# Two graph layers on one core: four small re-orderings at the seams of the stages

## Chip, cores, metric

One core of one Trainium2 chip runs the whole program; the other cores are idle. The metric is the device time of one execution in microseconds (us), as a median of several runs. Below, the engines are called TensorE (PE in the profile), VectorE (DVE), ScalarE (ACT), GpSimd (POOL) and SyncE (SP). SyncE computes nothing: it issues DMA transfers. ScalarE and GpSimd can issue transfers too, each in its own instruction stream.

## What is computed

The inputs are `x` (8 batches, 2048 rows, 256 columns, float32) and a sparse 2048 x 2048 matrix `adj` with a full diagonal. Cut to what matters, the reference is:

```python
# layer 0
deg   = rowsum(adj + I) + colsum(adj + I) - diag(adj + I)
A_hat = (adj + I) * deg**-0.5 [rows] * deg**-0.5 [columns]
h   = relu(batchnorm((A_hat @ x) @ W1.T))        # 512 columns, statistics over all 16384 rows
x   = layernorm(x + batchnorm(h @ W2.T))         # back to 256 columns
# layer 1
q, k, v = split(x @ W)                           # 4 heads of 64
attn = softmax(q @ k.T / 8, only where adj != 0)
x   = layernorm(x + attn @ v)
```

## The kernel before, in words

The 2048 rows are cut into 16 row tiles of 128. Rows with low numbers have many neighbours, the others few. So row tiles 0 and 1 of layer 0, and row tile 0 of layer 1, are done densely; every other row tile goes through lists of its neighbours' numbers: rows of the neighbours are gathered from DRAM by indirect DMA and added up with weights. Five stages follow one another. A recording layer (`manual_schedule`) keeps, on each engine, the order in which the Python program emits instructions, so every engine is a queue in that order.

**Stage 1, column sums and searches (lines 425 to 478).** For each row tile `t`, SyncE loads 128 rows of `adj` into a slot `e` (1 MB; there are 16 slots). ScalarE adds up its rows (L432) and its diagonal (L433), TensorE adds its columns into the PSUM tile `pc` by a product with ones (L451). For `t > 2` the loop also takes two steps from the generator `search_steps`. A search of one row tile is four steps, all on VectorE: it replaces nonzeros of the slot by their column numbers (L224), finds the eight largest of each of 12 or 16 segments (L230, in two steps), and merges these (L235 to L242) into a list of up to 32 neighbours, `nbx`. There are 15 searches, 60 steps: row tiles 2 to 15, then 1. After the loop VectorE copies `pc` to SBUF (`cs`, L464), TensorE transposes it (L467), VectorE combines row sums, diagonal and column sums (L468 to L470), and GpSimd raises the result to the power -1/2 (L146): `dinv`. Then `list_steps` for row tiles 2 and 3 turns the merged lists into gather indices, alternating between VectorE and small TensorE products (L258 to L321, L269, L287).

**Stage 2, dense products (lines 483 to 506).** For each of 16 row blocks `m`, SyncE loads `x` of all batches into `xt` (four buffers), ScalarE scales it by `dinv` (L489) and issues its store to the scratch `xs_d` (L490), and TensorE multiplies it into eight PSUM banks (L493). Each pass takes three more search steps from the generator while any are left, and one or two gathers of `adj` values for the lists of tiles 2 and 3 (L327, GpSimd).

**Stage 3 (to about 600 us)** gathers rows of `xs_d` (L565), adds them up on VectorE (L643) and TensorE (L652), and makes the first linear layer (L393), kept or stored as `h_d`.

**Stage 4 (to about 814 us)** is the second linear layer (`second_linear`), for 16 pairs of row blocks. Pair `n` gives two tiles, `Y[n][0]` and `Y[n][1]`; `store_y(n, r)` stores each with four transfers of 128 KB into the scratch `y_d`, issued by SyncE as soon as VectorE has finished the tile (L738). The order of pairs is 12 to 15, then 0 to 11. So the last pair belongs to blocks 2, 6, 10 and so on of `y_d`. Behind the last stores SyncE issues the loads of the next stage: `wq` (L823), `bias0` (L825), then `yt` from block 0 of `y_d` (L893) and `x1` (L895).

**Stage 5, layer 1 (from about 814 us to the end).** Layer 1's input is normalised and projected for two batches at a time (four such pairs of batches, `p` = 0 to 3; queries, keys and values go to DRAM). A long loop over `n` (4 x 131 = 524 passes) then handles one list entry of 128 rows per pass. Its parts are staggered: pass `n` scores entry `n + 5` (VectorE, L1233 and L1235), takes exponentials of `n + 4` (ScalarE, L1244), weighs the values of `n + 3` (`wv`, on ScalarE by eight instructions at L1260 or on VectorE by one at L1265), and adds up entry `n` for one batch and `n - 2` for the other in PSUM (`add_up`, L1276). The sums `po` of a row tile come from the pool `ps_o`, which has three buffers; the pool `ps_m`, four buffers called `pm`, serves everything else. Other work is hung into the passes by number with `at(n, f, ...)`. When row tile `t` of batch `b` is complete, its tasks are `finish` (divide by the sum of weights, VectorE, L1087 and L1089, which frees the `po` buffer), `residual` (GpSimd, L1096), `out_stats` (VectorE, L856 and L858). After four row tiles (a chunk of 512 rows) come `out_root` (GpSimd, L144 and L146), `out_shift` (VectorE, L866), and `emit` in two halves (ScalarE, two applications L872 each); the second half also issues the store of the whole chunk (512 KB, L1129). In the last pair of batches the entries 518 to 523 form row tile 15, entries 512 to 517 row tile 14. At the very end a small count decides whether a fallback must run (L1357 to L1364, the value is read by all engines at L1677); with these inputs it doesn't.

Of the kernel before, what the change touches and what calls it, by code (L numbers as in the profile page):

```python
# [8 lines left out]
F32 = mybir.dt.float32  # L9
# [9 lines left out]
NHEADS = 4  # L19
# [23 lines left out]
def tile_gcn_then_masked_attention(  # L43
# [15 lines left out]
    nc = tc.nc  # L59
    ENG = mybir.EngineType  # L60
    PSUM = bass.MemoryType.PSUM
    P = 128
# [352 lines left out]
    with tc.tile_pool(name="first", bufs=1, side="right") as fp, tc.manual_schedule(  # L415
        engines=ALL4
    ):
        at = fp.tile([P, DENSE, NT, P], F32, name="at")
        rsum = fp.tile([P, NT], F32, name="rsum")
        diag = fp.tile([P, NT], F32, name="diag")  # L420
        with tc.tile_pool(name="pst", bufs=4, space=PSUM) as pst, tc.tile_pool(
            name="psc", bufs=1, space=PSUM
        ) as psc:
            pc = psc.tile([P, CH], F32, name="pc")
            for t in range(NT):
                s = rows_of[t] = Slot()
                a = s.t
                nc.sync.dma_start(a, adj[t * P : (t + 1) * P, :])
                dj = fp.tile([P, P], F32, name="dj")
                nc.gpsimd.tensor_mul(dj, a[:, t * P : (t + 1) * P], ident)  # L430
                junk = fp.tile([P, N], U8, name="junk")
                nc.scalar.activation(junk, a, AF.Copy, accum_out=rsum[:, t : t + 1])  # L432
                nc.scalar.activation(dj, dj, AF.Copy, accum_out=diag[:, t : t + 1])  # L433
                if t < DENSE:
                    for g in range(NT // 4):
                        ps = pst.tile([P, 4, P], F32, name="ps")
                        for i in range(4):
                            mt = 4 * g + i
                            nc.tensor.transpose(ps[:, i, :], a[:, mt * P : (mt + 1) * P], ident)
                        nc.vector.tensor_copy(at[:, t, 4 * g : 4 * g + 4, :], ps)  # L440
                    if not t:
                        for half in range(2):
                            here = slice(half * NT // 2, (half + 1) * NT // 2)
                            mb = fp.tile([P, NT // 2, P], BF16, name="junk")
                            nc.vector.tensor_scalar(
                                mb, at[:, 0, here], 0.0, MASKED, op0=ALU.is_equal, op1=ALU.mult
                            )
                            nc.sync.dma_start(bias_d[:, here], mb)
                    nc.gpsimd.tensor_add(at[:, t, t, :], at[:, t, t, :], ident)
                for c in range(NCH):  # L450
                    nc.tensor.matmul(  # L451
                        pc[32 * c : 32 * (c + 1), :], ones[:, :32], a[:, c * CH : (c + 1) * CH],
                        start=(t == 0), stop=(t == NT - 1),
                    )
                if not t:
                    rows_of.pop(0).done()
                if t > 2:
                    for _ in range(2):
                        next(search)
            nc.sync.dma_start(w1s, w1t.rearrange("(c p) f -> p c f", p=P))  # L460
            for dst, src in params:
                nc.sync.dma_start(dst, src)
            cs = fp.tile([P, CH], F32, name="junk")
            nc.vector.tensor_copy(cs, pc)  # L464
            pt = psc.tile([P, TPC, P], F32, name="pt")
            for i in range(TPC):
                nc.tensor.transpose(pt[:, i, :], cs[:, i * P : (i + 1) * P], ident)  # L467
            nc.vector.tensor_scalar(over[:, 2, :], diag, 0.0, None, op0=ALU.is_equal)  # L468
            nc.vector.scalar_tensor_tensor(rsum, rsum, 1.0, diag, op0=ALU.add, op1=ALU.subtract)
            nc.vector.tensor_add(  # L470
                rsum.rearrange("p (j i) -> p i j", i=TPC),
                pt.rearrange("p i (j r) -> p i j r", j=NCH)[:, :, :, 0],
                rsum.rearrange("p (j i) -> p i j", i=TPC),
            )
            rsqrt(dinv, rsum, NT, 0.0)
            for t in (2, 3):
                for _ in list_steps(t, pst, "ps"):
                    pass

        ps_a = right.enter_context(tc.tile_pool(name="ps_a", bufs=1, space=PSUM))  # L480
        with tc.tile_pool(name="ps_b", bufs=1, space=PSUM) as ps_b:
            pa = [banks(p) for p in (ps_a, ps_b)]
            for m in range(NT):
                xt = fp.tile([P, N], F32, name="xt", bufs=4)
                nc.sync.dma_start(
                    xt.rearrange("p (b d) -> p b d", b=B),
                    x[:, m * P : (m + 1) * P, :].rearrange("b p d -> p b d"),
                )
                nc.scalar.activation(xt, xt, AF.Copy, scale=dinv[:, m : m + 1])  # L489
                nc.scalar.dma_start(xs_d[m * P : (m + 1) * P, :], xt)  # L490
                for t in range(DENSE):
                    for c in range(QC):
                        nc.tensor.matmul(  # L493
                            pa[t][c], at[:, t, m, :], xt[:, c * CH : (c + 1) * CH],
                            start=(m == 0), stop=(m == NT - 1),
                        )
                for _ in range(3):
                    next(search, None)
                if m < ELL[2] + CAP[2]:
                    gather_value(col0[2] + m)  # L500
                if m < ELL[3] + CAP[3]:
                    gather_value(col0[3] + m)
            for t in (2, 3):
                weights(t)
            for t in range(DENSE):
                scale_rows(t, pa[t])
# [173 lines left out]
    with tc.tile_pool(name="l1", bufs=1, side="right", reuse_waits="tile") as lp, tc.tile_pool(  # L680
# [60 lines left out]

        def store_y(n, r):
            c, i = divmod(pairs[n][0] // 2, TPC)
            for b in range(B // 2):
                nc.sync.dma_start(
                    y_d[(r * B // 2 + b) * NCH + c][:, :, i * P : (i + 1) * P],
                    Y[n][r][:, :, b * P : (b + 1) * P],
                )
# [130 lines left out]
    def attention():  # L879

        with ExitStack() as st:
# [240 lines left out]
            def emit(b, c, half):  # L1122
# [5 lines left out]
                here = slice(parts(b, c)[0], TPC)  # L1128
                nc.sync.dma_start(rows(b, c, out)[:, here], x1.pop((b, c))[:, here])  # L1129

            def emit_rest(b):
                lo.pop((b, "rest")).apply([0])
                nc.sync.dma_start(out[b, :P, :], rest.pop(b)[:, 0, :])
# [137 lines left out]
            def add_up(n, b):  # L1271
                p, g = divmod(n, NG)
                t, r, col, e = tiles[g]
                if not r:
                    po[p, t, b] = ps_o.tile([P, NHEADS, VW], F32, name="po")
                nc.tensor.matmul(  # L1276
                    po[p, t, b].rearrange("p h e -> p (h e)"), oh[n] if e >= 0 else ident,
                    wv[n][:, b, :], start=(r == 0), stop=(r == ELL[t] + CAP[t] - 1),
                )
                if b:  # L1280
                    del wv[n]
                    oh.pop(n, None)
# [39 lines left out]
            for n in range(NALL_G):  # L1322
                p, g = divmod(n, NG)
                t, r, _, _ = tiles[g]
                if n + AHEAD < NALL_G:
                    score(n + AHEAD)
                if n + AHEAD - 1 < NALL_G:
                    exps(n + AHEAD - 1)
                if n + AHEAD - 2 < NALL_G:
                    weigh_values(n + AHEAD - 2)  # L1330
                if n > 1:
                    add_up(n - 2, 1)
                add_up(n, 0)
                if n + LEAD < NALL_G:
                    gather(n + LEAD)
                side_tasks(n)
                if r == ELL[t] + CAP[t] - 1:
                    for b in range(G2):
                        u = n + 1 + 2 * b
                        at(u, finish_block, p, t, b)  # L1340
                        at(u + 1, residual, p * G2 + b, t)
                        at(u + 3, out_stats, p * G2 + b, t)
                        if t % TPC == TPC - 1:
                            u = n + 6 + 2 * b
                            at(u, out_root, p * G2 + b, t // TPC)
                            at(u + 1, out_shift, p * G2 + b, t // TPC)
                            for half in range(2):
                                at(u + 2 + half, emit, p * G2 + b, t // TPC, half)
# [375 lines left out]
```

## Time and profile before

| what | value |
|---|---|
| median of 3 runs | 2200.36 us (2194.45 to 2200.84) |
| the profiled execution's own time | 2182.95 us |
| span of that execution, first to last instruction | 2181.2 us |
| mean granted TensorE clock in it | 0.945 |
| busy: TensorE, VectorE, ScalarE, GpSimd | 1932.5 us (89%), 1735.4 (80%), 1381.4 (63%), 1438.4 (66%) |
| `adj` row tile 15 added into the column sums (L451 ends) | 58.7 us |
| dense products L493 | 88.64 to 200.3 us |
| last product of stage 4 ends, first `yt` load of stage 5 issued | 813.1 us, 817.33 us |
| last list product ends | 2165.6 us |

A row of the timeline gives start (us), duration (us), engine, line, operation, out<-in with shapes, a count, and in brackets how long the engine sat idle before it and what ended the wait. A row of the chain of waits gives start, duration and what the end of the program was waiting for in that stretch. A row of the table by stretches gives, for a stretch of time, the busy time of the five engines with counts of instructions, the TensorE clock that was granted (1.00 is full), the mean busy share of the 16 DMA engines, and GB/s. "SPq" and "ACTq" are the sequencers of SyncE and ScalarE issuing a transfer; "PEld" is TensorE's load of weights.

### The profile page before, as it was taken

How to read it: one execution, taken by the hardware profiler on the slowest of the kernel's cores; microseconds unless marked ns; L12 is line 12 of the kernel's file. 1: busy time of each engine (PE TensorE's matmuls, PEld its weight loads, DVE VectorE, ACT ScalarE, POOL GpSimd, SP SyncE). 2: the span in 40 equal slices, each digit the busy share in tenths (PEclk: the TensorE clock that was granted, in tenths of full speed). 3: DMA queues.
4: the chain of work that ended last, by engine and by line, in shares of the span. 5: the costliest groups of instructions: out<-in, count | busy, mean ns of one | idle time of the engine just before them, and what ended most of it. 6: DMA issues, size and time to landing. Idle time of an engine off the chain costs nothing.

```text
span 2181.2 us, 27900 instructions
## 1 busy us (share of the span) xinstructions
PE 1932.5 (89%) x7590; PEld 1256.5 (58%) x7590; DVE 1735.4 (80%) x3537; ACT 1381.4 (63%) x4145; POOL 1438.4 (66%) x1417
## 2 busy tenths in 40 slices
PE   5599979899999997989999999989999999778785
PEld 1244444454434435657776777767777777566663
DVE  6862898889766662249899998899998999978896
ACT  6222322233354535658878888878797888789886
POOL 2322688888367761146778876777885877777884
PEclk7699989999999998989999999999999999899987
DMA  8698999999738435578999999999998999999994
GB/s 319 198 309 346 414 348 366 371 377 403 298 119 284 157 104 196 198 282 308 347 357 341 354 337 352 351 326 359 329 365 335 344 348 355 364 348 343 336 361 156
DMA packets 259335, 681.89 MB, mean 313 GB/s; under 512 B 25952, under 2 KB 125024, under 8 KB 234208
## 3 DMA queue, kind: packets, MB, share of 16 engines
q0 software_dynamic: 106896, 434.28, 53.2%
q1 hardware_dynamic: 149968, 228.96, 29.9%
q10 hardware_dynamic: 2304, 16.78, 1.8%
q8 instruction: 63, 1.03, 0.2%
q14 instruction: 104, 0.85, 0.1%
HBM read 553.31 MB, written 126.62 MB: 312 GB/s over the span
## 4 chain that ended last, share of the span: by engine, by line
PE 48%; DVE 19%; ACT 13%; DMA 9%; issue 6%; POOL 4%; SPq 0%; another core or an unknown queue 0%; DVEq 0%; ACTq 0%; POOLq 0%
PE pm L1000 9%; PE pa L721 8%; PE po L1276 7%; PE ph L393 7%; ACT wv L1260 6%; PE pa L493 5%; DVE pr L1233 4%; PE pa L652 3%; DVE wv L1265 3%; DVE s L1235 2%; ACT x L872 2%; DMA e<-xs_d,idx 2%; DMA x<-in_x_dram 2%; DMA kg<-kv_d,idx 2%; PE pm L1049 2%
## 5 line engine op out<-in xcount | busy, mean ns | idle before, releaser
L1215 POOL DMA_INDIRECT kg<-kv_d,idx x524 | 558.9, 1067 | 151.4 <-issue 99.5
L1260 ACT ACTIVATE wv<-kg,pw 128x65 f32<-128x65 f32 x1880 | 473.5, 336 | 3.6 <-issue 1.9
L1276 PE MATMUL po<-wv,ident 128*128 128x260 f32 x1536 | 432.9, 395 | 37.1 <-DVE z L1089 18.4
L1000 PE MATMUL pm<-wq,x1t 128*128 128x512 f32 (+1 forms) x1024 | 375.5, 497 | 13.8 <-ACT x1t L945 9.4
L1235 DVE TENSOR_REDUCE s<-pr 128x8 f32<-128x512 f32 x524 | 359.4, 686 | 34.5 <-issue 0.5
L1276 PEld LDWEIGHTS po<-wv,ident 128*128 128x128 f32 x1536 | 286.5, 196 | 101.5 <-issue 52.1
L1233 DVE TENSOR_TENSOR pr<-qb,kg 128x512 f32<-128x512 f32 x384 | 272.5, 710 | 8.6 <-DMA kg<-kv_d,idx 4.1
L1000 PEld LDWEIGHTS pm<-wq,x1t 128*128 128x128 f32 x1024 | 186.8, 193 | 107.0 <-issue 76.5
L565 POOL DMA_INDIRECT e<-xs_d,idx x115 | 158.8, 1381 | 114.9 <-DMA xs_d<-xt 61.7
L1244 ACT ACTIVATE pw<-s,padb 128x8 f32<-128x8 f32 x524 | 155.3, 298 | 119.0 <-DVE s L1235 91.8
L393 PE MATMUL ph<-e,w1s 128*128 128x512 f32 x512 | 226.8, 594 | 1.7 <-ACT e L411 0.9
L1265 DVE TENSOR_TENSOR wv<-kg,pw 128x520 f32<-128x520 f32 x289 | 209.9, 726 | 20.0 <-PE po L1276 13.6
L327 POOL DMA_INDIRECT av<-in_adj_dram,fidx x115 | 164.5, 1431 | 45.5 <-issue 31.4
L1276 PE MATMUL po<-wv,oh 128*128 128x260 f32 x560 | 174.4, 397 | 2.1 <-ACT wv L1260 1.1
L1221 POOL DMA_INDIRECT qg<-q_d,idxq x140 | 141.2, 1008 | 42.7 <-issue 42.4
L398 ACT ACTIVATE h<-ph,b1s 128x512 f32<-128x512 f32 x96 | 66.0, 687 | 156.8 <-PE ph L393 139.1
L643 DVE SCALAR_TENSOR_TENSOR e<-e,wgt,e 128x2048 f32<-128x2048 f32 x70 | 163.9, 2341 | 0.2
L393 PEld LDWEIGHTS ph<-e,w1s 128*128 128x128 f32 x512 | 95.6, 190 | 114.7 <-issue 110.5
L1068 PEld LDWEIGHTS po<-kvr,p 128*128 128x128 f32 x1024 | 136.6, 196 | 43.0 <-ACT p L1057 22.8
L1096 POOL TENSOR_TENSOR x<-z,x 128x256 f32<-128x256 f32 x126 | 125.7, 999 | 51.6 <-DVE z L1089 43.4
L1068 PE MATMUL po<-kvr,p 128*128 128x65 f32 x1024 | 134.1, 275 | 28.2 <-ACT p L1057 19.8
L1049 PE MATMUL pm<-q,kt 128*128 128x256 f32 x512 | 139.3, 396 | 9.5 <-issue 4.7
(193 smaller groups left out, 3298.0 us busy)
## 6 DMA issues: line engine op xcount, KB each, us to landing
kv_d<-kvr SPq DMA_DIRECT2D x32, 1032.0 KB
h_d<-h SPq DMA_DIRECT2D x24, 1024.0 KB
e<-h_d SPq DMA_DIRECT2D x24, 1024.0 KB
e<-in_adj_dram SPq DMA_DIRECT2D x16, 1024.0 KB
xt<-in_x_dram SPq DMA_DIRECT2D x16, 1024.0 KB
xs_d<-xt ACTq DMA_DIRECT2D x16, 1024.0 KB
y_d<-y SPq DMA_DIRECT2D x128, 128.0 KB
yt<-y_d SPq DMA_DIRECT2D x32, 512.0 KB
```

The costliest lines, as they stand in the source:

```text
L327: nc.gpsimd.indirect_dma_start(out=av[:, col : col + 1], out_offset=None, in_=adj_flat, in_offset=bass.IndirectOffsetOnAxis(ap=fidx[:, col ...
L393: nc.tensor.matmul(ph, w1s[:, d, f * P : (f + 1) * P], as_agb(agb[t])[:, d, r * B // 2 : (r + 1) * B // 2, :], start=(d == 0), stop=(d == ...
L721: nc.tensor.matmul(py, w[:, f, :], t[:, f, :], start=(f == 0), stop=(f == 1))
L1000: nc.tensor.matmul(pm, x1t[b, c][:, d, i * P : (i + 1) * P], rhs(d), start=(d == 0), stop=(d == ND - 1),)
L1049: nc.tensor.matmul(pm[:, hp].rearrange("p r q -> p (r q)"), k[:, hp, :], q0[b][:, hp].rearrange("p r q -> p (r q)"), start=False, stop=Tru ...
L1068: nc.tensor.matmul(po0[b][:, h, :], p[:, h, :], heads(kvr[b, c][:, i, D:])[:, h, :], start=(j == 0 and h == 0), stop=(j == NT - 1), skip_g ...
L1215: nc.gpsimd.indirect_dma_start(out=kg[n].rearrange("p b e -> p (b e)"), out_offset=None, in_=kv_d[p][:], in_offset=bass.IndirectOffsetOnAx ...
L1233: nc.vector.tensor_mul(pr, q, kg[n][:, :, :D])
L1235: nc.vector.tensor_reduce(s.rearrange("p b h -> p (b h)"), pr.rearrange("p b (h e) -> p (b h) e", e=HD), AX.X, ALU.add,)
L1260: nc.scalar.activation(wv[n][:, b, hs], k[:, b, D:][:, hs], AF.Copy, scale=w[:, b, h : h + 1],)
L1265: nc.vector.tensor_mul(wv[n].rearrange("p b (h e) -> p b h e", e=VW), k[:, :, D:].rearrange("p b (h e) -> p b h e", e=VW), w[:, :, :, None ...
L1276: nc.tensor.matmul(po[p, t, b].rearrange("p h e -> p (h e)"), oh[n] if e >= 0 else ident, wv[n][:, b, :], start=(r == 0), stop=(r == ELL[t ...
```

## The change

There are four edits.

1. In stage 1 the loop takes one search step for even `t` and two for odd `t`, instead of two always: for `t` from 3 to 15 that is 20 steps instead of 26. The other six are taken by the passes of stage 2, which take three each until all 60 are done. The copy of the column sums `pc` to `cs` moves from VectorE to ScalarE.
2. The eight stores of the last pair's `Y` tiles are issued by ScalarE and not by SyncE.
3. In the last pair of batches (`p == NP - 1`), the sums of row tiles 14 and 15 are placed in the pool `ps_m` and not in `ps_o`.
4. The last chunk of the last pair of batches is normalised and stored in two halves of two row tiles: root, shift, two applications and a store of 256 KB, all emitted at one pass, five passes (seven for the second batch) after row tile 13 and again after row tile 15.

```diff
                 if t > 2:
-                    for _ in range(2):
+                    for _ in range(1 + t % 2):
                         next(search)
...
             cs = fp.tile([P, CH], F32, name="junk")
-            nc.vector.tensor_copy(cs, pc)
+            nc.scalar.copy(cs, pc)
...
         def store_y(n, r):
             c, i = divmod(pairs[n][0] // 2, TPC)
+            queue = nc.scalar if n == len(pairs) - 1 else nc.sync
             for b in range(B // 2):
-                nc.sync.dma_start(
+                queue.dma_start(
...
+            def emit_half(b, c, half):
+                mine = range(IT * half, IT * (half + 1))
+                lo[b, c].root(mine)
+                lo[b, c].shift(mine)
+                lo[b, c].apply(mine)
+                here = slice(mine[0], mine[-1] + 1)
+                nc.sync.dma_start(rows(b, c, out)[:, here], x1[b, c][:, here])
...
                 if not r:
-                    po[p, t, b] = ps_o.tile([P, NHEADS, VW], F32, name="po")
+                    at_end = p == NP - 1 and t >= NT - IT
+                    po[p, t, b] = (ps_m if at_end else ps_o).tile(
+                        [P, NHEADS, VW], F32, name="pm" if at_end else "po"
+                    )
...
-                        if t % TPC == TPC - 1:
+                        if p == NP - 1 and t // TPC == NCH - 1:
+                            if t % IT:
+                                half = t % TPC // IT
+                                at(n + 5 + 2 * b, emit_half, p * G2 + b, t // TPC, half)
+                        elif t % TPC == TPC - 1:
```

Here `NT` is 16, `TPC` 4, `IT` 2, `NCH` 4. On VectorE the change takes L224 to L242 of row tile 7, and L224 with nine of the sixteen L230 of row tile 8, from in front of L468 to behind `list_steps` of row tile 3.

## Prediction

> **What bounds the kernel now.** The page's busy shares (TensorE 89%, VectorE 80%) say little about four edits at the seams of stages, so I read each seam: first the chain of waits over the span, to see who holds it there, then the timeline rows, then the table by stretches for what lies behind.
>
> Seam A, end of stage 1. Timeline:
>
> ```profile
> 64.26 0.29 DVE L239 MAX8 nbx<-best 128x8 f32<-128x128 f32 x1
> ...
> 75.27 0.68 DVE L464 COPY junk<-pc 128x512 f32<-128x512 f32 x1
> ...
> 76.01 1.12 PE L467 MATMUL pt<-ident,junk 128*128 128x128 f32 x4 [17.28 <-DVE junk L464]
> 77.16 0.18 DVE L470 TENSOR_TENSOR rsum<-pt,rsum 128x16 f32<-128x16 f32 x1 [1.05 <-PE pt L467]
> ...
> 80.44 2.00 ACT L489 ACTIVATE xt<-xt,dinv 128x2048 f32<-128x2048 f32 x1 [21.32 <-POOL dinv L146]
> ...
> 88.64 31.84 PE L493 MATMUL pa<-xt,at 128*128 128x512 f32 x70 [1.17 <-DVE junk L297]
> ```
>
> The last column sum ends on TensorE at 58.7 (L451: 56.79 + 1.94). Everybody then waits for VectorE: TensorE 17.28 us, ScalarE 21.32 us. The copy L464 depends only on the column sums, but stands behind the searches, which the chain names without a gap from 27.9 to 75.4. Row tile 6's search ends at 64.5, row tile 7's at 71.7. Stages by stretches:
>
> ```profile
> 60.00:80.00 20.00, 1.83 (x7) 1.41 (x8) 17.52 (x68) 0.00 (x0) 2.51 (x1) 0.50 0.65 208
> 160.00:180.00 20.00, 20.00 (x48) 8.77 (x47) 0.00 (x0) 6.26 (x4) 0.00 (x0) 1.00 0.88 314
> ```
>
> VectorE is the engine before 80, TensorE fills its time after; VectorE has nothing from 147.08 to 195.19 (L360's row shows 48.11 us idle).
>
> Seam B, stage 4 to 5. Chain of waits:
>
> ```profile
> 813.99 0.14 DVE ident L824
> 814.13 0.40 SPq L745
> ...
> 816.66 0.62 SPq L825
> 817.28 0.04 issue
> 817.33 6.35 DMA yt<-y_d
> ```
>
> SyncE issues four stores (814.02 for 2.60 us), then `bias0`, then the load that everyone needs, which takes 6.35 us.
>
> Seam C, the end. Timeline:
>
> ```profile
> 2158.10 2.01 ACT L1260 ACTIVATE wv<-kg,pw 128x65 f32<-128x65 f32 x8
> ...
> 2158.37 2.07 PE L1276 MATMUL po<-wv,ident 128*128 128x260 f32 x4 [4.41 <-DVE z L1089]
> ...
> 2168.64 4.04 ACT L872 ACTIVATE x<-x,lo_nm,lo_rs 128x256 f32<-128x256 f32 x8 [8.53 <-DVE lo_nm L866]
> ...
> 2170.74 2.34 SPq L1129 DMA_DIRECT2D out_dram<-x  x2
> ```
>
> TensorE waits 4.41 us for VectorE to free a `po` buffer; eight applications of 0.5 us stand before the last store.
>
> **Edit 1, searches and copy.** VectorE's queue loses, ahead of L468, row tile 7's search (64.47 to 71.74, 7.27 us), row tile 8's two steps (71.74 to 75.36, 3.62) and the copy (0.60 net of overlap). The copy on ScalarE costs what ScalarE's PSUM copy of that shape costs at L729, 0.58 us; its queue is free at 59.1 (last L433 row: 58.93 + 0.19), so `cs` is there at 59.8 and the transposes (1.12) end at 61.0, before VectorE gets to L468 at 64.47. L468 and L469 take 0.09 each, so L470 starts at 64.7 and not at 77.16: **12.5 us earlier**. From there to the first dense product the path is the same (`dinv`, two list builds, 77.16 to 88.64 = 11.5 us), so products start at 76.2. Cover needed: `xt` loads. The loads of the first four blocks are issued from 57.8 on, and by the DMA queues' rows all traffic ends at about 72.2, so four blocks are in by then; ScalarE scales the first at 68.0 to 70.0, product one needs it at 76.2, product block four at about 97. Later loads wait for a product to free a buffer, so they move along.
>
> The six steps now lie in stage 2, 10.9 us of VectorE. Before, VectorE worked on from 89.6 to 147.1; after, from 77.2 to 77.2 + 10.9 + 57.5 = 145.6. Next due is L360 at 195.2 - 12.5 = 182.7: 37 us of cover, cost nothing. All of stage 3 follows from stage 2 (its first gather waits for `xs_d`), so the shift is carried. Value 12.45; bounds 11.5 (a slower first TensorE transposes, contention of the earlier `xs_d` stores with the last loads) and 12.7.
>
> **Edit 2, stores by ScalarE.** Eight issues leave SyncE; ScalarE has 20.38 us of idle before L900, so they delay nothing there (its next work waits for `yt`). `wq` still waits for the last product at 813.07 (that row is not moved), so `bias0` goes at 813.65 and `yt` at 814.3 instead of 817.33: 3.0 us by the issue rows. Against it stands the row of the DMA engines:
>
> ```profile
> 818.00:819.00 1.00, 0.00 (x0) 0.00 (x0) 0.20 (x2) 0.00 (x0) 0.00 (x0) 0.50 1.19 350
> ```
>
> They are between 0.80 and 1.19 busy in every microsecond from 813 to 826 (second figure from the end). [...] By the issue rows 3.0. The stores may fall behind the loads, as nobody waits for them before batch 0's third chunk; I take 1.5, keeping 0 and 3.0. Normalisation constants (L165, done 818.1) are not in the way. The projection after it is held by TensorE and carries the shift.
>
> **Edits 3 and 4, the tail.** With own buffers, entry 518's second product no longer waits for L1089 at 2158.22; it could go at 2154. But then the next wait comes last: `wv` of entry 522, on ScalarE until 2160.11, with five products behind it. And edit 4 puts two pairs of applications (0.98 us a pair) in ScalarE's queue, one before `wv` 520, one before the exponentials of 523 and `wv` 522. Each of these waits for a shift, placed in VectorE's queue behind GpSimd's root of the same pass; GpSimd is idle there (7.33 us before L1096), root takes 1.3 us, and VectorE has 1.4 us or more of other work between, so the two shifts cost it 0.1 to 0.4 us each. Walking ScalarE's queue through: `wv` 520 ends 1.0 later at 2157.3, the second pair waits for the shift at 2158.0 and ends at 2159.0, exponential and one-hot 1.0, `wv` 522 ends at **2161.9**, 1.8 later.
>
> Five products from there. Before, ten products took 7.25 us, since the granted clock was 0.50 after the idle stretch; at full clock two take 0.87 (2163.70, 1.04 with the drain). [...] At full clock the last product ends at 2164.1, at half clock at 2166.4; before 2165.6. I take the middle, 2165.2: 0.4 us gained.
>
> After it: `residual`, root of two tiles, shift, two applications instead of eight for the store. But VectorE's statistics of batch two now stand behind batch one's shift, which waits for GpSimd: about +1.2. From last product to last store issue: 7.1 us before (2165.6 to 2172.7), about 5.8 after. Yet SyncE's read of the fallback flag follows the store, and the flag's count moves only 0.5 later, so I count 0.9 of it. Tail 1.3; bounds 3.0 gained and 1.0 lost.
>
> **Sum.** 12.45 + 1.5 + 1.3 = 15.2 us. Against the profiled execution's own 2182.95 us: 2167.7. That execution lies 17.4 below the median of the runs, with a span of 2181.2 plus 1.75 around it; the shift is in fixed stretches, so on the median it gives 2200.4 - 15.2 = **2185**.
>
> **Rivals.** (a) *Only seam A pays*: DMA bytes hold seam B, the tail loses 1: 12.4 + 0 - 1 = 11.4, 2189 us. For it: the DMA row and ScalarE's queue; against: 3 us of free issue. Chance 0.22. (b) *A's gain is half absorbed by loads*: if the earlier gathers and stores slow the first `xt` blocks until TensorE waits for a fifth block, 5 to 7 us remain, 2194. Against: the fifth block's scaling at 103.65 was 13 us ahead of its products. Chance 0.09. (c) *Slower*: the six moved steps make the searches the end of stage 2. Place: VectorE's queue before L360. It decides once its stage 2 work grows by 37 us, and passes the old time at 37 + 15 = 52; 59 us would be 2207. Only if searches beside GpSimd's gathers ran nearly twice as long; the rows of L230 in 92 to 110 (2.95 to 3.19 us) are those of stage 1 (2.80 to 3.19). Chance 0.04. (d) *Forecast*: 0.65.
>
> **Numbers.** Runs of before spread over 6.4 us, and 0.3% (6.6 us) is about what a measurement of this kernel can tell from no change: faster means under 2193.8. Forecast and (a) are faster unless the runs stray: 0.85; (b) gives most of same: 0.11; slower 0.04. Range: bounds of the sum are 10.5 to 18.7 gained, 2182 to 2190; with (b) and the runs' spread, 2175 to 2194.
>
> **What would show it.** L470 near 64.7, L493 near 76.2, its end near 187.9, VectorE idle from about 146; first `yt` load issued near 814.3 - 12.5, its wait under 6.35; in the tail no TensorE wait for L1089, `wv` 522 late. Wrong if L464's copy, `xt` or L493 waits for a load, or stage 3 gives the shift back.

## The result, and the profile after

| | us |
|---|---|
| changed kernel, median of 5 runs | 2180.85 (2174.72 to 2189.74) |
| kernel before in the same set, median of 5 runs | 2195.52 (2190.72 to 2200.84) |
| ratio, 95% interval | 0.9921, 0.9899 to 0.9944 |
| profiled execution of the changed kernel, its span | 2185.41, 2183.6 |

By the ratio the change takes 12 to 22 us off 2200; the forecast took 15.2 off and said 2185. The two profiled executions alone would mislead: 2182.95 before, 2185.41 after. The difference between them lies in the loop over list entries, which the change touches only at its very end: from its first sum to its last gather it took 1178.4 us in the one and 1196.0 in the other. So everything below is read seam by seam.

Seam A. Timeline of the changed kernel (start, duration, engine, line; in brackets the idle time ahead and its cause):

```profile
58.64 0.56 ACT L464 COPY junk<-pc 128x512 f32<-128x512 f32 x1
59.26 1.12 PE L467 MATMUL pt<-ident,junk 128*128 128x128 f32 x4 [2.12 <-ACT junk L464]
62.77 0.29 DVE L239 MAX8 nbx<-best 128x8 f32<-128x128 f32 x1
63.31 0.18 DVE L470 TENSOR_TENSOR rsum<-pt,rsum 128x16 f32<-128x16 f32 x1
66.60 2.00 ACT L489 ACTIVATE xt<-xt,dinv 128x2048 f32<-128x2048 f32 x1 [7.40 <-POOL dinv L146]
74.78 1.19 PE L493 MATMUL pa<-xt,at 128*128 128x512 f32 x1 [1.17 <-DVE junk L297]
```

The copy is done on ScalarE and the transposes end at 60.38, while VectorE still searches row tile 6; L470 starts a quarter of a microsecond after that search has ended (62.77 + 0.29), without a wait for TensorE. ScalarE's wait for `dinv` is 7.40 us, 21.32 before. The price of the move shows in stage 2, by stretches and in L360's row:

```profile
140.00:160.00 20.00, 20.00 (x48) 8.88 (x47) 3.54 (x18) 5.43 (x4) 0.00 (x0) 1.00 0.92 305
160.00:180.00 20.00, 20.00 (x48) 8.79 (x47) 0.00 (x0) 3.29 (x2) 5.25 (x6) 1.00 0.73 270
```

```profile
181.95 0.75 DVE L360 TENSOR_SCALAR e<-pa,dinv 128x512 f32<-128x512 f32 x1 [37.96 <-PE pa L493]
```

TensorE is full in both stretches, VectorE runs dry at 144 and waits 37.96 us for it, 48.11 before: the moved steps came out of this idle time.

Seam B. Timeline of SyncE's queue, then the chain of waits:

```profile
789.63 5.87 SPq L746 DMA_DIRECT2D y_d<-y  x7
795.62 0.54 SPq L824 DMA_DIRECT2D wq<-in_L_gnn_W_dram  x1
803.31 0.33 SPq L826 DMA_DIRECT2D bias<-bias_d  x1
804.64 0.32 SPq L894 DMA_DIRECT2D yt<-y_d  x1
```

```profile
804.63 0.03 DVE ident L825
804.66 5.58 DMA y_d<-y
810.24 1.51 ACT yt L901 x2
```

The last product of stage 4 ends at 803.71. `yt` is asked for 0.9 us later (4.3 before), and ScalarE can start on it 5.58 us after that (6.35 before). The chain puts this wait down to a store that ended with it. In e12 below, with the same edit, the chain of waits names the load itself:

```profile
801.85 4.32 DMA yt<-y_d
```

`wq` has left 8 us before the last product (795.62 against 803.71).

Seam C. Timeline of the end:

```profile
2161.08 1.23 PE L1288 MATMUL pm<-wv,ident 128*128 128x260 f32 x2 [0.67 <-ACT wv L1269]
2164.70 2.01 ACT L1269 ACTIVATE wv<-kg,pw 128x65 f32<-128x65 f32 x8
2165.80 0.71 PE L1288 MATMUL pm<-wv,oh 128*128 128x260 f32 x2 [0.93 <-ACT wv L1269]
2170.83 0.42 DVE L857 BATCH_NORM_STATS2 lo_st<-x 128x6 f32<-128x256 f32 x1
2174.40 0.15 DVE L1380 TENSOR_SCALAR bad<-pm 1x1 int32<-1x1 f32 x1 [0.37 <-PE pm L1379]
```

TensorE no longer waits for L1090 (L1089 before); what it waits for in these last products are weighed values on ScalarE. The last row is the count, by now the end of the chain.

### The profile page after: what moved, and what is told of

Its sections match the earlier page's. It is cut to its first block, busy times and chain, and to the rows that moved or that the text cites. A ratio compares the mean times of both kernels' runs of the same rounds, so it can differ in the third digit from the quotient of the medians.

```text
span 2183.6 us, 27909 instructions
## 1 busy us (share of the span) xinstructions
PE 1936.5 (89%) x7590; PEld 1258.8 (58%) x7590; DVE 1734.6 (79%) x3538; ACT 1380.9 (63%) x4146; POOL 1447.2 (66%) x1421
## 4 chain that ended last, share of the span: by engine, by line
PE 46%; DVE 19%; ACT 16%; issue 7%; DMA 7%; POOL 4%; another core or an unknown queue 1%; DVEq 0%; SPq 0%; POOLq 0%; ACTq 0%
PE pm L1001 9%; PE pa L721 8%; ACT wv L1269 8%; PE ph L393 7%; PE po L1288 6%; PE pa L493 5%; DVE pr L1242 5%; PE pa L652 4%; DVE wv L1274 3%; DVE s L1244 3%; ACT x L873 3%; DMA e<-xs_d,idx 2%; PE po L1069 2%; POOL kg L1224 2%; PE pm L1050 1%
## 5 line engine op out<-in xcount | busy, mean ns | idle before, releaser
L1288 PE MATMUL po<-wv,ident 128*128 128x260 f32 x1504 | 423.7, 394 | 24.5 <-DVE z L1090 16.7
L1288 PEld LDWEIGHTS po<-wv,ident 128*128 128x128 f32 x1504 | 279.7, 196 | 86.4 <-issue 41.5
L565 POOL DMA_INDIRECT e<-xs_d,idx x115 | 163.7, 1423 | 116.2 <-DMA xs_d<-xt 62.6
L393 PE MATMUL ph<-e,w1s 128*128 128x512 f32 x512 | 226.8, 594 | 1.6 <-ACT e L411 0.8
L1230 POOL DMA_INDIRECT qg<-q_d,idxq x140 | 142.1, 1015 | 42.7 <-issue 42.4
L1288 PE MATMUL po<-wv,oh 128*128 128x260 f32 x544 | 168.5, 395 | 0.9 <-ACT wv L1269 0.9
L393 PEld LDWEIGHTS ph<-e,w1s 128*128 128x128 f32 x512 | 95.6, 190 | 114.6 <-issue 111.2
```

The costliest lines, as they stand in the source:

```text
L393: nc.tensor.matmul(ph, w1s[:, d, f * P : (f + 1) * P], as_agb(agb[t])[:, d, r * B // 2 : (r + 1) * B // 2, :], start=(d == 0), stop=(d == ...
L565: nc.gpsimd.indirect_dma_start(out=xg[n].t, out_offset=None, in_=xs_d[:], in_offset=bass.IndirectOffsetOnAxis(ap=idx[:, col : col + 1], ax ...
L1288: nc.tensor.matmul(po[p, t, b].rearrange("p h e -> p (h e)"), oh[n] if e >= 0 else ident, wv[n][:, b, :], start=(r == 0), stop=(r == ELL[t ...
```

## Experiments

Twelve kernels ran in three sets, each with its own runs of the kernel before: medians 2197.05 (e1 to e4), 2172.46 (e5 to e8) and 2173.98 us (e9 to e12). The sets differ by 1%, all kernels alike, mostly in the loop over list entries (1178 to 1196 us up to e4, 1165 to 1170 from e5 on), so ratios are taken inside a set only. This table is worked out from the starts and ends of rows in each trace; "A" is the time from the L224 that opens row tile 5's search to the first dense product L493, "stage 3" from the end of L493 to that of L393, "B" from the end of stage 4's products to the first transposition of `yt`, "wv" and "end" from the last gather to the last weighed values on ScalarE and to the end of the span. Columns are us.

| kernel | ratio to before | A | stage 3 | B | wv | end |
|---|---|---|---|---|---|---|
| before | 1 | 38.89 | 413.36 | 11.57 | 13.80 | 34.91 |
| changed | 0.9921 | 26.33 | 417.25 | 7.38 | 15.66 | 32.55 |
| e1, edit 1 | 0.9946 | 26.35 | 417.20 | 11.39 | 13.92 | 34.36 |
| e2, edit 2 | 0.9979 | 38.69 | 414.51 | 7.26 | 13.79 | 33.31 |
| e3, edit 3 | 0.9981 | 38.69 | 414.13 | 11.59 | 13.80 | 32.00 |
| e4, edit 4 | 0.9999 | 38.87 | 414.73 | 11.59 | 16.02 | 34.80 |
| e5, edit 1, copy on VectorE | one run | 27.89 | 413.51 | 11.42 | 13.80 | 34.45 |
| e6, half of edit 2 | one run | 38.70 | 414.73 | 9.18 | 13.80 | 34.62 |
| e7, changed, again | 0.9939 | 26.34 | 417.49 | 7.58 | 15.68 | 32.73 |
| e8, mended | 0.9908 | 22.76 | 417.69 | 7.59 | 13.80 | 30.92 |
| e9, changed, copy on VectorE | 0.9916 | 27.89 | 412.94 | 7.42 | 15.66 | 34.11 |
| e10, maxima twice | one run | 26.35 | 413.95 | 7.66 | 15.67 | 32.58 |
| e11, maxima three times | one run | 26.57 | 455.71 | 7.49 | 15.67 | 32.78 |
| e12, edits 1 to 3 | 0.9904 | 26.76 | 413.80 | 6.43 | 13.79 | 32.33 |

### e1 to e4: each edit alone

The diffs are those of the change, one edit each.

> Edit 1 alone (20 search steps beside the column sums, the copy of the sums by ScalarE). Theory S (each edit pays at its own seam, the rest of the program only moves along): L470 12 to 13 us earlier after the sixth row tile's search than before, first dense product with it, stage 2 as long as before (111 to 113 us), time 12 us below before. Theory L (the shifted start makes the long loop of layer 1 longer, as the profiled execution after has 1196 us from first sum to last gather against 1178): loop again near 1196 us, time within 5 us of before.

> Edit 2 alone (last pair's stores by ScalarE). Theory S, as the profile after shows it: the load of wq leaves the queue place behind the last pair's first stores and is issued some 17 us before the last product of stage 4, yt follows about 1 us after that product, from that product to the first transposition of yt 7.4 us instead of 11.6: 4.2 us gained. The forecast's own working (only issue time, wq not moved): 1.5 us. Theory L: loop longer by over 10 us.

> Edit 3 alone (sums of row tiles 14 and 15 in the other pool). TensorE's wait of 4.4 us for the freed buffer goes; the last weighed values on ScalarE end as before, 13.8 us after the last gather is issued; five products at full clock follow (2.2 us): last product 16 us after the last gather instead of 19.3, so 3 us gained; at half clock 4.5 us and 1 us gained.

> Edit 4 alone (last chunk's norm in halves). If ScalarE's queue decides: last weighed values 1.8 us later than before after the last gather (15.6 us instead of 13.8), but TensorE waits for the freed buffer anyway, so the last product is 0 to 1 us later, and from it to the end 0.3 to 1 us less: no change beyond 1 us. If the shorter norm pays in full: 1.5 us or more gained.

Measured ratios with 95% intervals: e1 0.9946 (0.9923 to 0.9968), e2 0.9979 (0.9966 to 0.9991), e3 0.9981 (0.9960 to 1.0001), e4 0.9999 (0.9984 to 1.0014). In us of 2197: 11.9, 4.6, 4.2 and 0.2 gained, 20.9 in all, inside the 12 to 22 of the whole change. So edit 1 is most of it, and edit 2 is worth more than the forecast gave it. Edit 3 is the gain at the end: its interval just reaches 1, but its profile ends 32.00 us after the last gather, and the five profiles that have neither edit 3 nor edit 4 end after 33.31 to 34.91. Edit 4 is nothing: its own price, `wv` 2.2 us later, is in its trace.

Theory L falls. The loop over list entries took 1185.9, 1194.4, 1188.3 and 1185.5 us in e1 to e4, whichever edit was in, and 1169.6 us with the whole change in e7. (The "17 us" in e2's expectation is a slip: `wq` leaves 8 us before the last product, in the changed kernel as in e2.)

### e5: the steps without the copy

```diff
                     for _ in range(1 + t % 2):
...
-            nc.scalar.copy(cs, pc)
+            nc.vector.tensor_copy(cs, pc)
```

(against e1's form of edit 1)

> Edit 1 without the copy to ScalarE: the three fewer search steps of the odd row tiles up to 7 and the step of tile 8's place leave VectorE's queue as in the change, but the copy L464 stays on VectorE behind row tile 6's searches. Forecast's working (the copy counted 0.60 us net plus the transposes behind it): the two-element add L470 stands 7.60 us after row tile 6's query row is scaled for the searches in the changed kernel, 20.15 in the kernel before; here it should stand at about 7.6 + 0.6 + 1.6 (copy, hand-over to TensorE, transposes) = 9.5, so that about 10.6 of seam A's 12.5 us come from the steps and about 2 from the copy. Rival (the copy is what matters, since TensorE waits for it): 15 or later, half of the gain lost.

```profile
55.84 2.27 DVE L224 SCALAR_TENSOR_TENSOR e<-e,down 128x2048 f32<-128x2048 f32 x1
63.11 0.67 DVE L464 COPY junk<-pc 128x512 f32<-128x512 f32 x1
64.99 0.18 DVE L470 TENSOR_TENSOR rsum<-pt,rsum 128x16 f32<-128x16 f32 x1 [1.05 <-PE pt L467]
```

L470 stands 9.15 us after row tile 6's L224 (7.60 in the changed kernel, 20.15 before): the steps are 11.0 of the 12.55 us, the copy 1.55. The rival (15 or later) falls. (What edit 1 takes away are six steps, one at each even `t` from 4 to 14; "three" and "odd" in the expectation are slips.)

### e6: half of edit 2

```diff
-            queue = nc.scalar if n == len(pairs) - 1 else nc.sync
+            queue = nc.scalar if n == len(pairs) - 1 and r else nc.sync
```

(edit 2 alone otherwise)

> Edit 2 for one of the two row tiles of a pair alone: the first row tile's stores of the last pair stay in SyncE's queue, so wq stands behind a store that waits for the last product again, which is the situation that the forecast assumed. If the gain of seam B comes from wq getting away early (and not from the issue time of the stores), the gap from the last product of stage 4 to the first transposition of yt comes back to 10 to 11.5 us (11.57 before, 7.26 with edit 2 whole), wq is issued after the last product and gains 0 to 1.5 us. Rival, issue time alone: four of eight issues are gone, so half of the 4.3 us is kept, the gap about 9.4.

Here `wq` does leave behind the last product, as the forecast had assumed for the whole change. Chain of waits:

```profile
813.77 0.03 SPq L824
...
813.84 0.54 SPq L824
...
814.42 0.50 SPq L826
814.93 0.34 issue
815.26 6.79 DMA yt<-y_d
```

B is 9.18, where I had expected 10 to 11.5: my theory that the gain hangs on `wq` fell, and the issuing time of the stores alone (9.4 expected) held. `yt` is asked for 1.42 us after the last product (813.84) and not 4.26, 2.84 earlier, and the wait behind that takes 6.79 instead of 6.35. So with `wq` and `bias0` ahead of it and the stores beside it the load took back about 0.44 us of 2.84, no more. The other 1.8 us of edit 2 appear once the last four stores leave SyncE too and `wq` is away early: 0.5 in issue, 1.2 in the wait (6.79 to 5.58). This split rests on one profile of e6; B itself is 11.39 to 11.59 in the five profiles without edit 2, and with it 7.26 to 7.66 in seven and 6.43 in the eighth (e12).

### e7 and e9: is stage 3's 3 us real?

Edit 1's traces have a stage 3 of 417 us where those without it have 413 to 415.

> The changed kernel again, unaltered, for a second profile and second set of times. Stage 3 (from the end of the dense products to the last product of the first layer's networks) was 417.25 and 417.20 us in the two profiles that have edit 1, and 413.36 to 414.73 in the four that lack it. If edit 1 costs 3 us there in every execution, it is again 417; if the late gather of those two was chance, 413.4 to 414.7. The loop over the edges was 1178 to 1196 us in six executions of the same code; another value in that range. Ratio to the kernel before 0.990 to 0.994.

It was 417.49 again, so I looked at the copy, the one thing that e5 lacked. The diff of e9 is that of e5, in the whole change.

> The changed kernel with its copy of the column sums put back on VectorE (edit 1's fewer steps kept, edits 2 to 4 whole). In the one profile so far that has the fewer steps and the copy on VectorE, the dense products ended 0.8 to 1.0 us later than in the profiles with the copy on ScalarE, but stage 3 lasted 413.51 us, as in the five profiles without edit 1 (413.36 to 414.73), and not 417.2 to 417.7, as in all four that have the steps and the copy. Theory (stage 3 gives back 3 us when the products start as early as the copy on ScalarE lets them): stage 3 again near 413.5 to 414.7, so that it ends 1.5 to 3 us earlier than in the changed kernel, ratio to before equal or 0.001 lower. Rival (chance: the order in which gathers fall in stage 3's middle): stage 3 anywhere from 413 to 418, and the copy's 1.0 to 1.7 us lost in the total.

e9's stage 3 was 412.94, as that theory has it, and its ratio 0.9916 (0.9895 to 0.9936). But e12, with the copy on ScalarE, has 413.80, and e10 413.95. So the copy is not the cause. What is left is: of eight profiles with edit 1 (e11 left out, as its stage 3 starts late), four have 417.2 to 417.7 and four 412.9 to 414.0; all five without it have 413.4 to 414.7. The orders of instructions on all five engines are the same in stage 3. In the changed kernel the loss appears where VectorE waits for a value gather; the row is this one, there and in e12:

```profile
326.76 0.17 DVE L339 TENSOR_TENSOR wgt<-av,wgt 128x9 f32<-128x9 f32 x1 [10.21 <-DMA av<-in_adj_dram,fidx]
```

```profile
321.47 0.17 DVE L339 TENSOR_TENSOR wgt<-av,wgt 128x9 f32<-128x9 f32 x1 [5.17 <-DMA av<-in_adj_dram,fidx]
```

Without edit 1 this wait was 2.7 to 4.3 us, with it 4.3 to 10.2. It is not the whole loss: e1 waits 5.28 us here and has the long stage 3, e5 waits 5.79 and has the short one. Whether edit 1 makes the late order likelier or this is chance stays open.

### e10 and e11: how much VectorE work stage 2 hides

```diff
             for i, (u, v) in enumerate(zip(parts, parts[1:])):
-                nc.vector.max(out=best[:, i, :], in_=a[:, u:v])
+                for _ in range(2 if t >= 8 or t == 1 else 1):
+                    nc.vector.max(out=best[:, i, :], in_=a[:, u:v])
```

(3 in place of 2 for e11; the repeats write the same values again)

> The changed kernel with the segment maxima (L230) of row tiles 8 to 15 and 1 each taken twice (the second time for nothing): 3 x 3.19 + 6 x 2.95 = 27.3 us more for VectorE in stage 2. By the forecast's account of the slower case, VectorE has about 37 us of idle time there (37.96 before L360 in the changed kernel), so it costs nothing: 10.7 us idle stay before L360, dense products end as before, 112.2 after their start. Rival: searches beside the products slow gathers or products, and the stage ends later.

> The same with each of these maxima taken three times: 54.6 us more for VectorE in stage 2. Cover 37.96, so VectorE comes to L360 54.6 - 38.0 = 16.6 us late, TensorE waits for it at the first products of stage 3, and the whole is 14 to 17 us longer than the changed kernel's, about at the time of the kernel before (the forecast put the break-even at 52 us of added work). Rival: stage 3, which is bound by gathers in its first part, takes up half of it: 8 us.

The repeats cost more than their count. In the changed kernel a maximum starts before the one ahead of it has ended (at 138.73 for 0.33 us, the next at 138.98); in e10, where each repeat writes again what the one ahead of it wrote, the maxima stand apart: from 72 to 190 us, 4.5 us of idle time stand in front of 256 of them, against 0.3 in front of 136 in the changed kernel. Row tile 8's maxima in the changed kernel and in e10:

```profile
85.33 3.19 DVE L230 MAX8 best<-e 128x8 f32<-128x8 f32 x16
```

```profile
85.14 8.44 DVE L231 MAX8 best<-e 128x8 f32<-128x8 f32 x32
...
186.33 2.72 DVE L361 TENSOR_SCALAR e<-pa,dinv 128x512 f32<-128x512 f32 x4
```

e10 adds 38.5 us busy (65.75 against 27.25, the rows of row tiles 8 to 15 and 1) and 4.1 of gaps, 42.6 in all. That is more than the 38 us of cover, and VectorE comes to this row without a wait, but it still costs nothing: stage 3 is 413.95, the one run 2150.8 us, where e9 and e12 of the same set have medians of 2156.67 and 2154.26. The four scalings run back to back in 2.72 us, where the changed kernel spreads them over 5.9 as TensorE frees the banks. e11 adds 85.3 us by the same count:

```profile
231.00 2.71 DVE L361 TENSOR_SCALAR e<-pa,dinv 128x512 f32<-128x512 f32 x4
...
233.87 3.65 PE L411 MATMUL ph<-ident,e 128*128 128x128 f32 x16 [45.09 <-DVE over L264]
```

TensorE stands for 45.09 us, and the run takes 2194.93 us, 44.1 over e10. The size that I expected (14 to 17) was wrong because the added work was; by the measured work the account gives 85.3 - 42.6 = 42.7 us over e10. Both times are of one run each.

### e12: edits 1 to 3

```diff
-                        if p == NP - 1 and t // TPC == NCH - 1:
-                            if t % IT:
-                                half = t % TPC // IT
-                                at(n + 5 + 2 * b, emit_half, p * G2 + b, t // TPC, half)
-                        elif t % TPC == TPC - 1:
+                        if t % TPC == TPC - 1:
```

> Edits 1 to 3 without edit 4 (the last chunk's norm whole, as before). Theory: edit 4 takes back part of edit 3's gain, as its two extra pairs of applications stand in ScalarE's queue ahead of the last weighed values (15.7 us after the last gather instead of 13.8): here 13.8, the end 32.0 us after the last gather instead of 32.6 to 32.7, and the total 0.5 us below the changed kernel or equal to it, ratio to before 0.991 to 0.994. Rival: with edit 3 the halves do pay, and the end comes 33 us or more after the last gather.

Ratio 0.9904 (0.9885 to 0.9924), 32.33 us from the last gather to the end. It is not slower without edit 4. The traces have 32.55 to 32.78 us with edits 3 and 4 (34.11 in e9, where most of the last products ran at a granted clock of 0.50 to 0.52, up to 2138 us) and 32.00 and 32.33 with edit 3 alone; a price of half a microsecond for edit 4 would be less than the times can tell.

### e8: more of the one, less of the other

```diff
-                    for _ in range(1 + t % 2):
+                    for _ in range(1 + (t % 5 == 3)):
...
-                                at(n + 5 + 2 * b, emit_half, p * G2 + b, t // TPC, half)
+                                late_by = 0 if half else NALL_G - n - 6
+                                at(n + 5 + b + late_by, root_half, p * G2 + b, t // TPC, half)
+                                at(n + 7 + b + late_by, emit_half, p * G2 + b, t // TPC, half)
```

(`root_half` is the root taken out of `emit_half`; stage 1 takes 16 steps, four fewer than the changed kernel, so the "twelve" in the expectation is a slip)

> The change with more of the same and with its tail mended: in stage 1 twelve more... of the search steps go behind the column sums (a second step only for every fifth place), so that row tile 6's searches end sooner; in the tail the first half of the last chunk's norm is scaled behind the last weighed values, and the roots are called ahead of the shifts so that VectorE's statistics of batch two no longer stand behind batch one's shift. Theory: L470 stands about 2.9 us earlier than in the changed kernel (bound by TensorE's transposes, which were done 2.9 us before it), the last weighed values on ScalarE 13.8 us after the last gather instead of 15.7, the end about 31 us after the last gather instead of 32.6; in sum 4 to 5 us below the changed kernel, ratio to before about 0.990 against 0.992. Rival: the steps behind the sums now run past stage 2's end on VectorE, or the first norm half is on the path of the end: no gain.

```profile
58.55 0.17 DVE L468 TENSOR_SCALAR over<-diag 128x16 f32<-128x16 f32 x1 [2.10 <-ACT dj L433]
58.63 0.17 DVE L469 SCALAR_TENSOR_TENSOR rsum<-rsum,diag 128x16 f32<-128x16 f32 x1
60.19 0.18 DVE L470 TENSOR_TENSOR rsum<-pt,rsum 128x16 f32<-128x16 f32 x1 [1.39 <-PE pt L467]
```

Now VectorE waits for the column sums, as it should: A is 22.76, 3.6 us under the changed kernel, `wv` is back at 13.80, and the end comes 30.92 after the last gather. Ratio 0.9908 (0.9894 to 0.9922), in a set in which the changed kernel itself has 0.9939 (0.9916 to 0.9961): medians 2153.12 and 2159.86 us. The two intervals still overlap, so by the times alone e8 is not clear of the changed kernel; the gain is in the rows. e8 and e12 are the two lowest ratios; a kernel with both was not run.

## Why the prediction was right, and where its terms were not

**Seam A, 12.45 us: right.** Measured from the start of row tile 6's search, L470 came 12.55 earlier, and by column A the first product 12.56. The absolute times (63.31 for L470, 74.78 for L493, 187.06 for its end) lie 0.8 to 1.4 us before the forecast's because in this execution stage 1 itself ran 1.3 us earlier. `xt` was in time, the products took 112.28 us against 111.67.

**That stage 3 carries the shift: right in half of the profiles.** In the others it keeps 3 to 4 us of it. The forecast named this among the things that would make it wrong, but priced it at nothing; why half of the profiles lose it stays open.

**Seam B, 1.5 us: the mechanism was right, its size wrong.** Measured 4.2, above the upper bound of 3.0. The step that failed is the choice between the 3.0 us of the issue rows and the busy DMA engines: 1.5 was my estimate between 0 and 3.0, and no run shows it; half of edit 2 gave 2.39 (e6, B 9.18 against 11.57), the whole 4.2. e6 puts both to the test in the situation that the forecast described: 2.84 us of issue, of which the longer wait behind it took back 0.44. A DMA share of 0.80 to 1.19 in the rows was not evidence that the load would be held up: the load took 6.35 us there, 6.79 in e6 and 5.58 in the changed kernel. The second failed step is "`wq` still waits for the last product at 813.07 (that row is not moved)": `wq` had waited only because stores stood ahead of it in SyncE's queue. That its issue fell on the end of the last product was no dependence: the four stores ahead of it took SyncE's queue from 810.46 to 812.96. With the stores gone it left at 795.62, and this gave the other 1.8 us and broke the bound.

**The tail, 1.3 us: total near, both terms off.** Measured 2.4 from the last gather to the end, between the two profiles. This pair is a lucky one: the five profiles with the tail as before have 34.33 on average (33.31 to 34.91), the five with the whole change 32.95 (32.55 to 34.11), so 1.4. The last product was put 0.4 us earlier and came 2.1 earlier (17.21 after the last gather, 19.30 before), although `wv` of entry 522 came 1.86 later, as forecast (1.8). The term that I halved between two clocks was the reason: in the changed kernel the last products ran at full clock (1.00 from 2166 to 2168), in e9 mostly at half (0.52 from 2136 to 2138), and there they ended 18.67 after the last gather. Both ends were real, 1.5 us apart; the middle that I took is in neither trace. After the last product the forecast had 0.9 us gained, measured 0.28, and over the same ten profiles nothing (15.1 to 15.6 us with either tail): statistics of batch two do stand behind batch one's shift (L857 at 2170.83, the residual done at 2169.74), as forecast, and so the count, whose last row starts 6.1 us after the last product (5.9 before), is now what the end waits for.

**Sum.** Forecast 12.45 + 1.5 + 1.3 = 15.2. Measured by rows 12.55 + 4.2 + 2.4 = 19.1 (18.1 with the average tail), less up to 4 in stage 3: the undersized seam B and the unpriced loss cancelled. That the total came so near is luck in this part. The median's 2180.85 agrees, but it can't tell 15 from 19.

**The slower rival** needed 37 us more VectorE work in stage 2 to decide, and 52 for the old time. e10 hides 42.6 us. e11 is 21 us above its set's kernel before with 85.3, so the old time is passed near 64. The place was right, the cover was underestimated, since the four scalings, which can run back to back when late, and stage 3 behind them hide at least another 4.6 us.

## What to carry to other kernels

Steps of a long background task that stand in an engine's queue ahead of a value everybody waits for can be moved behind it as long as the next stage leaves that engine idle (here 48 us; whether stage 3 pays for part of it stayed open): read the idle time ahead of its first due instruction, and move until the producer of the value, not the queue, comes last (e8). When issues leave a queue, ask of each transfer behind them what it was really waiting for: it may go much earlier than the row beside it suggests. Two terms that cancel make a total look better understood than it is, so compare seam by seam, and distrust single profiles of a kernel whose long loop varies by more than 1%.

## What was not expected of the hardware

The same tail ends at two times, and in the two traces TensorE was granted its clock differently. TensorE's busy time is the second figure behind the stretch, the clock the third from the end. In the changed kernel:

```profile
2150.00:2151.00 1.00, 0.00 (x0) 0.00 (x0) 0.90 (x2) 0.41 (x2) 0.75 (x1) 1.00 0.93 372
2151.00:2152.00 1.00, 0.00 (x0) 0.00 (x0) 1.00 (x3) 0.66 (x3) 0.93 (x1) 0.52 1.10 367
...
2156.00:2158.00 2.00, 1.42 (x3) 1.18 (x4) 1.93 (x5) 1.97 (x8) 0.75 (x2) 0.50 0.12 36
2158.00:2160.00 2.00, 2.00 (x6) 1.35 (x4) 1.70 (x4) 2.00 (x8) 0.54 (x1) 0.50 0.00 1
2160.00:2162.00 2.00, 1.33 (x3) 0.82 (x3) 1.86 (x6) 2.00 (x10) 1.12 (x2) 0.50 0.39 131
2162.00:2164.00 2.00, 2.00 (x6) 1.43 (x6) 1.26 (x5) 1.40 (x5) 0.78 (x2) 0.50 0.01 4
2164.00:2166.00 2.00, 1.07 (x4) 0.38 (x3) 1.73 (x5) 1.97 (x9) 0.68 (x2) 0.83 0.38 131
2166.00:2168.00 2.00, 2.00 (x10) 1.62 (x9) 1.15 (x4) 0.71 (x3) 0.15 (x1) 1.00 0.00 0
```

and in e9:

```profile
2130.00:2132.00 2.00, 1.43 (x5) 0.83 (x5) 1.86 (x6) 1.39 (x7) 1.19 (x2) 0.77 0.36 122
2132.00:2134.00 2.00, 1.94 (x4) 1.01 (x4) 1.20 (x3) 1.97 (x6) 0.72 (x1) 0.50 0.04 13
2134.00:2136.00 2.00, 1.08 (x3) 0.89 (x4) 1.55 (x6) 1.82 (x8) 0.72 (x1) 0.50 0.35 118
2136.00:2138.00 2.00, 2.00 (x6) 1.59 (x5) 0.08 (x1) 0.00 (x0) 0.00 (x0) 0.52 0.00 0
2138.00:2140.00 2.00, 0.83 (x4) 0.38 (x2) 1.59 (x6) 0.00 (x0) 1.13 (x2) 1.00 0.00 0
```

In the changed kernel the granted clock fell from 1.00 to 0.52 at 2151 to 2152, was 0.50 from 2156 to 2164, 0.83 in the next 2 us and 1.00 in those from 2166 on, where most of the last group of products lies (2165.80 to 2168.26). In e9 it was 0.50 to 0.52 from 2132 to 2138 and 1.00 from there to 2140, and the last product ended at 2138.83. Four of these products took 1.04 us in the changed kernel (from 2166.35) and 1.94 in e9 (from 2135.94).

The half clock did not stand beside idle time alone. In the changed kernel it came in a pause of TensorE of 2.29 us (up to 2152.06), but stayed from 2156 to 2164, where TensorE was busy for 6.75 of 8 us. What makes the clock fall and come back at these places was not shown.
